# A three-engine score pipeline on one core: one more tile buffer, small steps moved between VectorE, ScalarE and GpSimd, and a new rule for which tiles are summed by DMA

## The chip, the core and the metric

The kernel runs on one core of a Trainium2 chip. The core has TensorE (PE, matrix products into PSUM), VectorE (DVE), ScalarE (ACT), GpSimd (POOL) and SyncE (SP, which here only issues DMAs), each with its own instruction queue, executed in order. They meet through semaphores. The time is device microseconds of one launch; the profile is of one such execution.

## The reference, cut to what matters

`x` is 64 batches of 256 nodes with 128 features, `adj` a 256x256 matrix. Four layers follow each other, each of the form `x = x + layer(relu(layernorm(x)))`. All is float32.

- Layer 0: a gated graph network of five steps. Each step mixes the nodes with `adj`, makes two sigmoid gates and a tanh candidate by 128x128 projections, and updates `h = (1 - z) * h + z * hv`.
- Layer 1: a Chebyshev product of `h`, `h @ adj` and a second hop with `Theta1`, then bias and relu.
- Layer 2: `(adj @ h + h) @ weight + bias`, divided by its norm per node.
- Layer 3: additive attention. For every pair of nodes (i, j) and all 256 channels it needs

```
pre  = s1[i] + s2[j] + b_lin
e    = sum over channels of leaky_relu(pre, 0.2) * a  + adj[i, j]
attn = softmax over j of e
out  = sigmoid(attn @ h)
```

The attention scores are nearly all of the elementwise work: 64 x 256 x 256 pairs with 256 channels each.

## The kernel before, in words

Batches are taken two at a time (32 pairs, `NB` = 2; the two batches of the first pair are started apart, "alone"). Three kinds of work are interleaved.

**Fronts** (`front`, one for each pair) do layers 0 to 2 and the preparation of layer 3. A front is a chain of small steps, each a Python generator's `yield` with the engine that does it. `norm` is the layer normalisation, called four times a front: statistics on VectorE, `1/sqrt(var + eps)` by two instructions on GpSimd (`inverse_root`, L391 and L392), the product -mean * that on VectorE (L469), and the scaled relu on ScalarE (L473). Each of the five recurrent steps has a tanh candidate on ScalarE (L601), `d - hT` on GpSimd (L605) and two updates on VectorE (L608, L612). Near its end a front makes the per-node value `s1o` on VectorE (L741) out of a small tile that VectorE has transposed (L739), and two rows, `lin` and `s2o`, that go to DRAM and come back spread over the partitions.

**Tiles.** The leaky relu is brought to a minimum or a relu of `s1[i] + s2[j]`. A slot is four rows i for both batches of a pair; there are 64 slots a pair, 2048 in all (`NSLOT`). Every slot needs two tiles of 128x2048 float32, one for each half of the 256 channels. The first half (k = 0) is made by VectorE in one instruction (L934) or by GpSimd in eight (L951); the second (k = 1) by ScalarE in eight (L946) or by GpSimd. The tiles live in a ring of 13 buffers, `rl0` to `rl12`. PE scores a tile with eight short matmuls recorded at L1010 (`score`), which add the channels with signs into a PSUM bank, and frees its buffer.

**Joined slots.** In 3 of 10 slots (`SHARE`, list `JOINED`: 614 of 2048, spread evenly to the last) the second half is always made by GpSimd, and a DMA that GpSimd issues (`add_pair`, L971) adds it into the first half's tile. PE then scores the sum once instead of two tiles. The buffer of the second half is free again when the DMA has landed, and the sum can be scored from then on.

**Tails** (`tail`, 64 of them: each half pair of 32 slots that has been scored) do the softmax: VectorE adds `min(s2o, s1o)` to the PSUM scores (L806), GpSimd adds the row `lin` (L818; VectorE in the last tail, L814), VectorE takes the maximum (L822), ScalarE the exponential (L826), PE transposes and multiplies by `h3`, VectorE inverts the sum (L846), ScalarE does the tanh that stands for the sigmoid (L851), and GpSimd the last two steps, `0.5 * o + 0.5` (L856) and `+ x3` (L857; VectorE in the last tail). Then SP sends the tile out.

**The order** of every engine's instructions is fixed when the program is built, by a planner in Python at the end of the function. It keeps a clock for each engine, gives each step an assumed duration (`ran`), and always extends the engine that is furthest behind: a step of a tail first, then one of a front, then, on PE a score and elsewhere a tile (on GpSimd an addition before a tile). So a tile goes to whichever engine has time. A front may not run ahead of a due time tied to the number of scores done:

```
due = STEPS_OF_FRONT * (scored[0] / (2 * SLOTS) - (key - 2)) / SPREAD
if CHAINS[key][2] > due + AHEAD:
```

so front `key` starts when the scores of pair `key - 2` begin and is spread over `SPREAD` = 1.7 pairs of scoring. The planner takes a DMA addition to last 6.6 us from its issue, and at least 5.3 us after the one before. At run time the engines keep the planned order, and wait where the plan was too early.

Of the kernel before, what the change touches and what calls it, by code (L numbers as in the profile page):

```python
# [14 lines left out]
P = 128  # L15
# [6 lines left out]
MOST_POSITIVE = -MOST_NEGATIVE  # L22
PE, DVE, ACT, POOL = ENGINES = (mybir.EngineType.PE, mybir.EngineType.DVE, mybir.EngineType.Activation, mybir.EngineType.Pool)
SLOTS = 64
SHARE = (3, 10)
AHEAD_OF = 2
LOW = 1
ISSUE, ADDED, LANDED, SLACK = 0.65, 5.3, 6.6, 0.3

# [2 lines left out]
def kernel(  # L32
# [122 lines left out]

    ident = const.tile([P, P], F32, name="ident")
    make_identity(nc, ident)
    place = work.tile([P, N], mybir.dt.int32, name="place", bufs=1)
    nc.gpsimd.iota(place, pattern=[[1, N]], base=0, channel_multiplier=0)
    feature = work.tile([P, NE], mybir.dt.int32, name="feature", bufs=1)  # L160
    nc.gpsimd.iota(feature, pattern=[[P, NE]], base=0, channel_multiplier=1)
# [13 lines left out]
    braw = const.tile([P, 5], F32, name="braw")  # L175
    for k, v in enumerate((w3_b, w4_b, w5_b, u3_b, u5_b)):
        nc.scalar.dma_start(braw[:, k:k + 1], v.rearrange("(p o) -> p o", o=1))
    th_raw = const.tile([P, 5, D], F32, name="th_raw")
    nc.sync.dma_start(th_raw, theta.rearrange("(k f) o -> f k o", f=P))
    w2 = const.tile([P, D], F32, name="w2")  # L180
    nc.sync.dma_start(w2, l2_weight)
# [18 lines left out]
    u3t, w4t, w3t, w5t = (wts[:, k] for k in range(4))  # L200
    w34 = const.tile([P, P], F32, name="w34")
    u5t = const.tile([P, P], F32, name="u5t")
    gate_b = const.tile([P, 3], F32, name="gate_b")
    bz, br, bh = gate_b[:, 0:1], gate_b[:, 1:2], gate_b[:, 2:3]
    th = th_raw[:, 0:3, :]
    win = const.tile([P, 63], F32, name="win")
    win_n = const.tile([P, 63], F32, name="win_n")
    w1 = const.tile([P, N], F32, name="w1")
# [6 lines left out]
    def first_constants():  # L215

        for c in range(NC):
            yield PE, 6.0, 1
            b = take()
            for k in range(NC):  # L220
                nc.tensor.transpose(b[0][:, k * P:(k + 1) * P], adj_n[:, k, c * P:(c + 1) * P], ident)
            t = ran(PE, 0.4, 6.0, b[1])
            yield DVE, t
            nc.vector.tensor_copy(adj_t[:, c, :], b[0][:, 0:N])
            t = ran(DVE, 0.35, t)
            spare.append([b[0], t])
# [228 lines left out]
    def norm(src, since, h):  # L455

        nb = src.shape[1]
        stats = work.tile([P, nb * NC, 3], F32, name="stats", bufs=4)
        mv = work.tile([P, nb * NC, 2], F32, name="mv", bufs=4)
        s, h = rows_of(src), rows_of(h)[:, :, 0:D]  # L460
        yield DVE, since
        for k in range(0, nb * NC, 2):
            nc.vector.bn_stats(stats[:, k:k + 2, :].rearrange("p k s -> p (k s)"), s[:, k:k + 2, :].rearrange("p k d -> p d k"))
        t = ran(DVE, STATS[nb], since)
        yield POOL, t
        inverse_root(mv[:, :, 1], stats[:, :, 2], 1.0 / D, OP.mult, LN_EPS, OP.add)
        t = ran(POOL, 1.45, t)
        yield DVE, t
        nc.vector.scalar_tensor_tensor(mv[:, :, 0], stats[:, :, 1], -1.0, mv[:, :, 1], op0=OP.mult, op1=OP.mult)  # L469
        t = ran(DVE, 0.1, t)  # L470
# [9 lines left out]
    def front(p, batches):  # L480
# [55 lines left out]
        for step in range(STEPS):  # L536
# [61 lines left out]
                t = ran(DVE, ELEMENTS[nb], t)  # L598
                spare.append([pv[0], t])
            else:  # L600
                nc.scalar.activation(d, seen(pv), AF.Tanh, bias=bh, scale=1.0)  # L601
                t = ran(ACT, TANH[nb], t)
                spare.append([pv[0], t])
                yield POOL, t
                nc.gpsimd.tensor_sub(d, d, hT)  # L605
                t = ran(POOL, 1.3, t)
            yield DVE, max(t, t_z)
            nc.vector.scalar_tensor_tensor(seen(pr), seen(pr), 1.0, d, op0=OP.add, op1=OP.mult)  # L608
            t = ran(DVE, ELEMENTS[nb], t, t_z)
# [84 lines left out]
        t = ran(POOL, 1.35, t)  # L694

        yield DVE, t, 0, lambda: p < 2 or (p - 2, NC - 1) in TAILED
        x3 = kept("x3", [NC, D])
# [7 lines left out]
        h3 = kept("h3", [NC, D + 1])  # L705
        nc.gpsimd.memset(h3[:, :, :, D:D + 1], 2.0)
        t = yield from norm(x3, t, h3)
        yield PE, t, 1
        b = take()
        to_feature(b[0], h3)  # L710
        t = ran(PE, TURN[nb], t, b[1])
        yield ACT, t
        hT = kept("hT3", [N])
        nc.scalar.copy(hT, seen(b))
        t_hT = ran(ACT, COPY[nb], t)
        spare.append([b[0], t_hT])
# [16 lines left out]
        quarter = work.tile([P, P], F32, name="quarter", bufs=2)  # L733
# [4 lines left out]
        turned = work.tile([P, P], F32, name="turned", bufs=2)  # L738
        nc.vector.transpose(turned[:, 0:cols], quarter[:, 0:cols])  # L739
        s1o = kept("s1o", [NC])  # L740
        nc.vector.tensor_scalar(s1o.rearrange("p b c -> p (b c)"), turned[:, 2:cols:32], b_odd, None, op0=OP.add)  # L741
        ran(DVE, 0.65, t)
# [56 lines left out]
    def tail(u, pe, since):  # L799
# [3 lines left out]
        yield DVE, max(since, ops["t_lin"])  # L803
        sc = feat("sc", **SHORT)
        for k, (b, c) in enumerate(across(u)):
            nc.vector.scalar_tensor_tensor(sc[:, k, :], ops["s2o"][:, b, :], ops["s1o"][:, b, c:c + 1], pe[k], op0=OP.min, op1=OP.add)  # L806
        t = ran(DVE, 0.8, since, ops["t_lin"])
        used = banks_of.pop(u)
        spare.append([used, t])
        end = u == (NPAIR - 1, NC - 1)  # L810
        more = lin.to_broadcast([P, NB, N]) if ops["alone"] else lin
        if end:
            yield DVE, max(t, ops["t_lin"])
            nc.vector.tensor_add(sc, sc, more)  # L814
            t = ran(DVE, ELEMENTS[2], t, ops["t_lin"])
        else:
            yield POOL, max(t, ops["t_lin"])
            nc.gpsimd.tensor_add(sc, sc, more)  # L818
            t = ran(POOL, 1.3, t, ops["t_lin"])
# [26 lines left out]
        nc.vector.reciprocal(rs, po[:, :, D])  # L846
        t = t_s = ran(DVE, 0.15, t)
        yield ACT, t
        o = work.tile([P, NB, D], F32, name="o")
        for k in range(NB):  # L850
            nc.scalar.activation(o[:, k, :], po[:, k, 0:D], AF.Tanh, scale=rs[:, k:k + 1])  # L851
        t = ran(ACT, 0.5, t, t_s)
        spare.append([bank[0], t])
        yield DVE if end else POOL, t
        e = nc.vector if end else nc.gpsimd
        e.tensor_scalar(o, o, 0.5, 0.5, op0=OP.mult, op1=OP.add)  # L856
        e.tensor_add(o, o, x3[:, 0] if ops["alone"] else x3[:, :, u[1], :])  # L857
        ran(DVE, 0.6, t) if end else ran(POOL, 1.2, t)
# [274 lines left out]
```

## Time and profile before

| what | value |
|---|---|
| median of 3 runs | 4924.24 us (4917.30 to 4930.92) |
| the profiled execution | 4930.46 us, its span 4928.2 us |
| busy PE / DVE / ACT / POOL | 97% / 96% / 94% / 95% of the span |
| tiles made by DVE / ACT / POOL | 1817 / 1261 / 1018 |
| joined slots, DMA additions | 614, median 7.8 us from issue to landing |
| granted TensorE clock, mean | 0.993 |

The profiled execution is 6.2 us over the median, and 2.3 us of it lie outside its span. Tiles are counted from instructions: one at L934 is a tile, eight at L946 or at L951 are one. In the groups of instructions a duration is from an instruction's start to its end. ScalarE, GpSimd and PE start the next before the last has ended, so the cost of one in a stream is read from the timeline: the length of an unbroken stretch by the number of instructions in it.

### The profile page before, as it was taken

What the parts mean: (1) busy time and instruction counts of PE and PEld (TensorE: products, weight loads), DVE (VectorE), ACT (ScalarE), POOL (GpSimd) and SP (SyncE); (2) the same over time, 40 slices, a digit from 0 to 9 for tenths busy, and PEclk for the clock granted to TensorE, in tenths of its full rate; (3) what the DMA queues carried; (4) which work ended last, traced back from release to release, by engine and by line L of the source; (5) the groups of instructions that cost most, each with busy time, mean ns of one, the idle gap of its engine ahead of it and who ended that gap; (6) DMA issues with size and microseconds to landing.
All of it is one profiled execution on the core that took longest, in us unless ns stands there. A gap on an engine that the chain in (4) does not pass through costs nothing.

```text
span 4928.2 us, 134012 instructions
## 1 busy us (share of the span) xinstructions
PE 4768.4 (97%) x52471; PEld 1739.2 (35%) x52471; DVE 4713.3 (96%) x3389; ACT 4643.9 (94%) x12142; POOL 4670.5 (95%) x9473
## 2 busy tenths in 40 slices
PE   9999999999999999999999999999999999999987
PEld 4333333333333333333333333333333333333322
DVE  5999999999999999999999999999999999999998
ACT  6999999999999989999999999999999999999998
POOL 3999999999999999999999999999999999999997
PEclk9999999999999999999999999999999999999999
DMA  1666766767767666776776666777767767767677
GB/s 40 137 141 132 151 138 132 148 136 146 144 134 149 138 141 138 143 147 134 145 152 137 142 140 138 148 143 143 144 130 147 148 139 144 144 137 143 143 155 148
DMA packets 133540, 687.45 MB, mean 139 GB/s; under 512 B 15144, under 2 KB 50344, under 8 KB 54312
## 3 DMA queue, kind: packets, MB, share of 16 engines
q0 software_dynamic: 88416, 643.86, 65.3%
q1 hardware_dynamic: 43768, 35.01, 2.3%
q8 instruction: 410, 6.72, 0.5%
q14 instruction: 226, 1.85, 0.1%
q10 hardware_dynamic: 720, 0.00, 0.0%
HBM read 26.48 MB, written 8.52 MB: 7 GB/s over the span
## 4 chain that ended last, share of the span: by engine, by line
PE 31%; POOL 18%; DVE 12%; DMA 7%; ACT 6%; issue 4%; POOLq 0%; ACTq 0%; DVEq 0%
PE bank L1010 19%; POOL rl L951 14%; PE bank L397 11%; DVE rl L934 10%; DMA rl<-rl 7%; ACT rl L946 5%; POOL rl L971 2%; POOL d L605 1%; PE bank L428 1%; POOL mv L392 1%; DVE mv L469 0%; DVE hT L612 0%; PE bank L420 0%; DVE bank L608 0%; POOL sc L818 0%
## 5 line engine op out<-in xcount | busy, mean ns | idle before, releaser
L934 DVE TENSOR_TENSOR rl<-s1a,bank 128x2048 f32<-128x2048 f32 x1817 | 4064.2, 2277 | 100.3 <-DMA rl<-rl 59.2
L946 ACT ACTIVATE rl<-bank,s1b 128x256 f32<-128x256 f32 x10088 | 4047.8, 819 | 113.6 <-DMA rl<-rl 62.8
L951 POOL TENSOR_SCALAR rl<-s2n,s1b 128x256 f32<-128x256 f32 x6296 | 2966.0, 668 | 50.6 <-DMA rl<-rl 19.2
L1010 PE MATMUL bank<-rl,win_n 128*32 128x512 f32 x17768 | 2211.3, 596 | 56.0 <-DVE rl L934 28.0
L1010 PE MATMUL bank<-rl,win 128*32 128x512 f32 x10088 | 1321.9, 597 | 0.0
L1010 PEld LDWEIGHTS bank<-rl,win_n 128*32 128x32 f32 x17768 | 557.2, 110 | 1215.1 <-issue 981.7
L951 POOL TENSOR_SCALAR rl<-s2c,s1a 128x256 f32<-128x256 f32 x1848 | 874.8, 643 | 7.1 <-DMA rl<-rl 2.5
L971 POOL DMA_DIRECT2D rl<-rl x614 | 575.6, 944 | 29.0 <-DVE rl L934 14.8
L1010 PEld LDWEIGHTS bank<-rl,win 128*32 128x32 f32 x10088 | 323.4, 110 | 655.5 <-issue 532.1
L397 PE MATMUL bank<-mT,wts 128*32 128x512 f32 x2480 | 326.2, 594 | 1.6 <-ACT mT L521 1.3
L397 PE MATMUL bank<-adj_t,h 128*32 128x256 f32 x4960 | 300.5, 381 | 7.5 <-ACT h L623 6.4
L605 POOL TENSOR_TENSOR d<-d,hT 128x512 f32<-128x512 f32 x155 | 228.7, 1475 | 37.8 <-ACT d L601 37.8
L397 PEld LDWEIGHTS bank<-adj_t,h 128*32 128x32 f32 x4960 | 159.6, 110 | 178.7 <-issue 46.6
L473 ACT ACTIVATE h<-x,mv 128x128 f32<-128x128 f32 x376 | 176.2, 720 | 13.5 <-DVE mv L469 13.2
L565 ACT ACTIVATE bank<-bank,gate_b 128x512 f32<-128x512 f32 (+1 forms) x165 | 148.5, 900 | 19.4 <-PE bank L397 14.3
L397 PE MATMUL bank<-mT,w 128*32 128x512 f32 x1240 | 163.3, 593 | 3.6 <-ACT bank L565 3.6
L397 PE MATMUL bank<-rh,u5t 128*32 128x512 f32 x1240 | 163.2, 592 | 2.3 <-DVE rh L569 2.3
L588 ACT ACTIVATE bank<-bank,gate_b 128x512 f32<-128x512 f32 (+1 forms) x165 | 154.0, 934 | 9.5 <-PE bank L397 9.4
L397 PE MATMUL bank<-hT,wts 128*32 128x512 f32 x1240 | 162.6, 593 | 0.0
L521 ACT COPY mT<-bank 128x512 f32<-128x512 f32 x155 | 137.1, 885 | 26.8 <-PE bank L397 24.8
L428 PE MATMUL bank<-ident,hT 128*128 128x128 f32 x620 | 101.7, 287 | 57.4 <-DVE hT L612 54.4
L601 ACT ACTIVATE d<-bank,gate_b 128x512 f32<-128x512 f32 x155 | 149.3, 963 | 3.6 <-PE bank L397 3.6
(204 smaller groups left out, 3494.8 us busy)
## 6 DMA issues: line engine op xcount, KB each, us to landing
rl<-rl POOLq DMA_DIRECT2D x614, 1024.0 KB, 7.8
rows<-row SPq DMA_DIRECT2D x31, 512.0 KB
xin<-in_x_dram SPq DMA_DIRECT2D x64, 128.0 KB
out_dram<-o SPq DMA_DIRECT2D x64, 128.0 KB
row<-quarter SPq DMA_DIRECT2D x62, 2.0 KB
rows<-row SPq DMA_DIRECT2D x2, 256.0 KB
w_raw<-in_L_gnn_w_w_dram SPq DMA_DIRECT2D x3, 128.0 KB
th_raw<-in_L_gnn_Theta_dram SPq DMA_DIRECT2D x1, 320.0 KB
```

The costliest lines, as they stand in the source:

```text
L397: nc.tensor.matmul(o[g:g + 32], w[:, g:g + 32], t, start=start, stop=stop, skip_group_check=True)
L428: nc.tensor.transpose(pt[:, b, c, :], ht[:, b, c * P:(c + 1) * P], ident)
L473: nc.scalar.activation(h[:, k, :], s[:, k, :], AF.Relu, bias=mv[:, k, 0:1], scale=mv[:, k, 1:2])
L565: nc.scalar.activation(seen(r), seen(pr), AF.Tanh, bias=br, scale=0.5)
L588: nc.scalar.activation(seen(pr), seen(pr), AF.Tanh, bias=bz, scale=0.5)
L601: nc.scalar.activation(d, seen(pv), AF.Tanh, bias=bh, scale=1.0)
L605: nc.gpsimd.tensor_sub(d, d, hT)
L934: nc.vector.tensor_tensor(t, rows.to_broadcast(whole), ops["s2a"].unsqueeze(1).to_broadcast(whole), op=OP.min)
L946: nc.scalar.activation(t[:, g, b, :], other(ops["s2p"][0], b), AF.Relu, bias=rows[:, g, b], scale=-1.0)
L951: nc.gpsimd.tensor_scalar(t[:, part, b, :], other(ops["s2n" if k else "s2c"], b), rows[:, part, b], MOST_NEGATIVE, op0=OP.min, op1=OP.max)
L971: nc.gpsimd.dma_start(out=t.rearrange("p g b n -> p (g b n)"), in_=z.rearrange("p g b n -> p (g b n)"), accum_op=OP.add)
L1010: nc.tensor.matmul(pe[g * 32:(g + 1) * 32, :], w[:, 31 - r:63 - r], flat(t[:, g]), start=False, stop=(left[u] == 0), skip_group_check=True)
```

## The change

- The ring has 14 tile buffers. Room for it: two set-up tiles (`place`, `th_raw`) lie in the first ring buffer until it is used, `th` becomes a tile of its own, two small tiles (`quarter`, `turned`) have one buffer instead of two, and the attention's turned input uses the `hT` ring of four instead of its own pair.
- Joined slots are 1 of 3 among the first 1952 slots, and none among the last 96: 650 instead of 614.
- `norm`: the sign change of the mean is a reduction over one element on VectorE, right behind the statistics, and the product is on GpSimd behind `inverse_root`. A step to VectorE and back is gone.
- `s1o` is a ScalarE activation (identity with bias) instead of a VectorE one.
- The recurrent candidate is made with its sign turned, so that GpSimd adds instead of subtracts, and the update has -0.5 for 0.5.
- `tail`: L806's result goes back into PSUM, and VectorE adds `lin` out of PSUM, for all tails. The tanh goes into PSUM, and one VectorE instruction does `0.5 * o + x3`. For this, GpSimd adds 0.5 to `x3` once a front, after the last `norm`.
- `SPREAD` is 1.8, and some assumed durations differ.

```diff
-SHARE = (3, 10)
+SHARE = (1, 3)
+ALONE = 96
+    tiles = [[relu_pool.tile([P, 4, NB, N], F32, name=f"rl{k}", bufs=1), 0.0] for k in range(14)]
+    scratch = tiles[0][0].rearrange("p g b n -> p (g b n)")
-    tiles = [[relu_pool.tile([P, 4, NB, N], F32, name=f"rl{k}", bufs=1), 0.0] for k in range(13)]
-    JOINED = [n for n in range(NSLOT) if (n + 1) * SHARE[0] // SHARE[1] > n * SHARE[0] // SHARE[1]]
+    JOINED = [n for n in range(NSLOT - ALONE) if (n + 1) * SHARE[0] // SHARE[1] > n * SHARE[0] // SHARE[1]]
...
+        nc.vector.tensor_reduce(mv[:, :, 0], stats[:, :, 1:2], AX.X, OP.add, negate=True)
         inverse_root(mv[:, :, 1], stats[:, :, 2], 1.0 / D, OP.mult, LN_EPS, OP.add)
-        t = ran(POOL, 1.45, t)
-        yield DVE, t
-        nc.vector.scalar_tensor_tensor(mv[:, :, 0], stats[:, :, 1], -1.0, mv[:, :, 1], op0=OP.mult, op1=OP.mult)
+        nc.gpsimd.tensor_mul(mv[:, :, 0], mv[:, :, 0], mv[:, :, 1])
...
-                nc.scalar.activation(d, seen(pv), AF.Tanh, bias=bh, scale=1.0)
+                nc.scalar.activation(d, seen(pv), AF.Tanh, bias=bh_n, scale=-1.0)
-                nc.gpsimd.tensor_sub(d, d, hT)
+                nc.gpsimd.tensor_add(d, d, hT)
-            nc.vector.scalar_tensor_tensor(hT_new, seen(pr), 0.5, hT, op0=OP.mult, op1=OP.add)
+            nc.vector.scalar_tensor_tensor(hT_new, seen(pr), 0.5 if alone else -0.5, hT, op0=OP.mult, op1=OP.add)
...
         t = yield from norm(x3, t, h3)
+        yield POOL, t
+        nc.gpsimd.tensor_scalar(x3, x3, 0.5, None, op0=OP.add)
-        hT = kept("hT3", [N])
-        nc.scalar.copy(hT, seen(b))
+        hT, t_hT = copied("hT", b, t, bufs=4)
...
-        nc.vector.tensor_scalar(s1o.rearrange("p b c -> p (b c)"), turned[:, 2:cols:32], b_odd, None, op0=OP.add)
+        nc.scalar.activation(s1o.rearrange("p b c -> p (b c)"), turned[:, 2:cols:32], AF.Identity, bias=b_odd, scale=1.0)
...
-            nc.vector.scalar_tensor_tensor(sc[:, k, :], ops["s2o"][:, b, :], ops["s1o"][:, b, c:c + 1], pe[k], op0=OP.min, op1=OP.add)
+            nc.vector.scalar_tensor_tensor(pe[k], ops["s2o"][:, b, :], ops["s1o"][:, b, c:c + 1], pe[k], op0=OP.min, op1=OP.add)
+        nc.vector.tensor_add(sc, by_feature(used), lin.to_broadcast([P, NB, N]) if ops["alone"] else lin)
-            nc.gpsimd.tensor_add(sc, sc, more)
...
-            nc.scalar.activation(o[:, k, :], po[:, k, 0:D], AF.Tanh, scale=rs[:, k:k + 1])
+            nc.scalar.activation(po[:, k, 0:D], po[:, k, 0:D], AF.Tanh, scale=rs[:, k:k + 1])
+        nc.vector.scalar_tensor_tensor(o, po[:, :, 0:D], 0.5, x3[:, 0] if ops["alone"] else x3[:, :, u[1], :], op0=OP.mult, op1=OP.add)
-        e.tensor_scalar(o, o, 0.5, 0.5, op0=OP.mult, op1=OP.add)
-        e.tensor_add(o, o, x3[:, 0] if ops["alone"] else x3[:, :, u[1], :])
...
-    STEPS_OF_FRONT, SPREAD, AHEAD = 109, 1.7, 2
+    STEPS_OF_FRONT, SPREAD, AHEAD = 109, 1.8, 2
```

More of the change, by code (lines that the diff above doesn't have):

```diff
@@ L157 @@
     make_identity(nc, ident)
-    place = work.tile([P, N], mybir.dt.int32, name="place", bufs=1)
+    place = scratch[:, 0:N].bitcast(mybir.dt.int32)
     nc.gpsimd.iota(place, pattern=[[1, N]], base=0, channel_multiplier=0)
@@ L177 @@
         nc.scalar.dma_start(braw[:, k:k + 1], v.rearrange("(p o) -> p o", o=1))
-    th_raw = const.tile([P, 5, D], F32, name="th_raw")
+    th_raw = scratch[:, N:N + 5 * D].rearrange("p (k o) -> p k o", k=5)
     nc.sync.dma_start(th_raw, theta.rearrange("(k f) o -> f k o", f=P))
@@ L202 @@
     u5t = const.tile([P, P], F32, name="u5t")
-    gate_b = const.tile([P, 3], F32, name="gate_b")
-    bz, br, bh = gate_b[:, 0:1], gate_b[:, 1:2], gate_b[:, 2:3]
-    th = th_raw[:, 0:3, :]
+    gate_b = const.tile([P, 4], F32, name="gate_b")
+    bz, br, bh, bh_n = (gate_b[:, k:k + 1] for k in range(4))
+    th = const.tile([P, 3, D], F32, name="th")
     win = const.tile([P, 63], F32, name="win")
@@ L255, in first_constants @@
         nc.vector.tensor_scalar(gate_b[:, 0:2], gate_b[:, 0:2], 0.5, None, op0=OP.mult)
+        nc.vector.tensor_scalar(bh_n, bh, -1.0, None, op0=OP.mult)
         ran(DVE, 0.3)
@@ L463, in norm @@
             nc.vector.bn_stats(stats[:, k:k + 2, :].rearrange("p k s -> p (k s)"), s[:, k:k + 2, :].rearrange("p k d -> p d k"))
-        t = ran(DVE, STATS[nb], since)
+        nc.vector.tensor_reduce(mv[:, :, 0], stats[:, :, 1:2], AX.X, OP.add, negate=True)
+        t = ran(DVE, STATS[nb], since) + 0.1
         yield POOL, t
         inverse_root(mv[:, :, 1], stats[:, :, 2], 1.0 / D, OP.mult, LN_EPS, OP.add)
-        t = ran(POOL, 1.45, t)
-        yield DVE, t
-        nc.vector.scalar_tensor_tensor(mv[:, :, 0], stats[:, :, 1], -1.0, mv[:, :, 1], op0=OP.mult, op1=OP.mult)
-        t = ran(DVE, 0.1, t)
+        nc.gpsimd.tensor_mul(mv[:, :, 0], mv[:, :, 0], mv[:, :, 1])
+        t = ran(POOL, 1.55, t)
         yield ACT, t
@@ L693, in front @@
         inverse_root(rn, rn, MOST_POSITIVE, OP.min, NORM_EPS * NORM_EPS, OP.max)
-        t = ran(POOL, 1.35, t)
+        t = ran(POOL, 1.35, t) + 0.1
         yield DVE, t, 0, lambda: p < 2 or (p - 2, NC - 1) in TAILED
@@ L707, in front @@
         t = yield from norm(x3, t, h3)
+        yield POOL, t
+        nc.gpsimd.tensor_scalar(x3, x3, 0.5, None, op0=OP.add)
+        ran(POOL, 0.45 if alone else 0.7, t)
         yield PE, t, 1
@@ L712, in front @@
         yield ACT, t
-        hT = kept("hT3", [N])
-        nc.scalar.copy(hT, seen(b))
-        t_hT = ran(ACT, COPY[nb], t)
-        spare.append([b[0], t_hT])
+        hT, t_hT = copied("hT", b, t, bufs=4)
         yield PE, t_hT, 1
@@ L732, in front @@
         yield ACT, t
-        quarter = work.tile([P, P], F32, name="quarter", bufs=2)
+        quarter = work.tile([P, P], F32, name="quarter", bufs=1)
         nc.scalar.copy(quarter[:, 0:cols], b[0][:, 0:cols])
@@ L737, in front @@
         yield DVE, t
-        turned = work.tile([P, P], F32, name="turned", bufs=2)
+        turned = work.tile([P, P], F32, name="turned", bufs=1)
         nc.vector.transpose(turned[:, 0:cols], quarter[:, 0:cols])
+        t_s = ran(DVE, 0.2, t)
+        yield ACT, t_s
         s1o = kept("s1o", [NC])
-        nc.vector.tensor_scalar(s1o.rearrange("p b c -> p (b c)"), turned[:, 2:cols:32], b_odd, None, op0=OP.add)
-        ran(DVE, 0.65, t)
+        nc.scalar.activation(s1o.rearrange("p b c -> p (b c)"), turned[:, 2:cols:32], AF.Identity, bias=b_odd, scale=1.0)
+        ran(ACT, 0.2, t_s)
         row = dram.tile([2, NB * N], F32, name="row", bufs=4)
@@ L805, in tail @@
         for k, (b, c) in enumerate(across(u)):
-            nc.vector.scalar_tensor_tensor(sc[:, k, :], ops["s2o"][:, b, :], ops["s1o"][:, b, c:c + 1], pe[k], op0=OP.min, op1=OP.add)
+            nc.vector.scalar_tensor_tensor(pe[k], ops["s2o"][:, b, :], ops["s1o"][:, b, c:c + 1], pe[k], op0=OP.min, op1=OP.add)
         t = ran(DVE, 0.8, since, ops["t_lin"])
+        yield DVE, t
         used = banks_of.pop(u)
+        nc.vector.tensor_add(sc, by_feature(used), lin.to_broadcast([P, NB, N]) if ops["alone"] else lin)
+        t = ran(DVE, ELEMENTS[2], t)
         spare.append([used, t])
[L810 to L817, printed above, removed]
-            nc.gpsimd.tensor_add(sc, sc, more)
-            t = ran(POOL, 1.3, t, ops["t_lin"])
         yield DVE, t
@@ L848, in tail @@
         yield ACT, t
+        for k in range(NB):
+            nc.scalar.activation(po[:, k, 0:D], po[:, k, 0:D], AF.Tanh, scale=rs[:, k:k + 1])
+        t = ran(ACT, 0.5, t, t_s)
+        yield DVE, t
         o = work.tile([P, NB, D], F32, name="o")
-        for k in range(NB):
-            nc.scalar.activation(o[:, k, :], po[:, k, 0:D], AF.Tanh, scale=rs[:, k:k + 1])
-        t = ran(ACT, 0.5, t, t_s)
+        nc.vector.scalar_tensor_tensor(o, po[:, :, 0:D], 0.5, x3[:, 0] if ops["alone"] else x3[:, :, u[1], :], op0=OP.mult, op1=OP.add)
+        t = ran(DVE, 0.36, t)
         spare.append([bank[0], t])
-        yield DVE if end else POOL, t
-        e = nc.vector if end else nc.gpsimd
-        e.tensor_scalar(o, o, 0.5, 0.5, op0=OP.mult, op1=OP.add)
-        e.tensor_add(o, o, x3[:, 0] if ops["alone"] else x3[:, :, u[1], :])
-        ran(DVE, 0.6, t) if end else ran(POOL, 1.2, t)
         p, k = u
```

## The prediction

> **What bounds the kernel now.** I read first the page's busy shares, then windows by stage, then the groups of instructions for what stands before the tiles, and last the timeline for prices and for the end.
>
> ```profile
> PE 4768.4 (97%) x52471; PEld 1739.2 (35%) x52471; DVE 4713.3 (96%) x3389; ACT 4643.9 (94%) x12142; POOL 4670.5 (95%) x9473
> ...
> 2000.00:3000.00 1000.00, 978.78 (x10728) 355.50 (x10720) 969.68 (x688) 956.59 (x2500) 976.01 (x1975) 1.00 0.70 143
> 4700.00:4800.00 100.00, 85.91 (x808) 26.70 (x800) 97.17 (x61) 99.94 (x273) 98.91 (x208) 0.97 0.80 164
> 4850.00:4900.00 50.00, 39.94 (x376) 11.38 (x372) 48.97 (x27) 50.00 (x141) 49.74 (x106) 1.00 0.78 159
> ```
>
> A window row has busy PE, PE's weight loads, DVE, ACT, POOL, then clock, DMA share, GB/s. No engine alone is the bound: in the middle all four are 96 to 98% busy. From 4700 us on (the fronts end at 4747) the three tile makers are full and PE is 80 to 86% busy: there a score saved is worth nothing.
>
> ```profile
> L934 DVE TENSOR_TENSOR rl<-s1a,bank 128x2048 f32<-128x2048 f32 x1817 | 4064.2, 2277 | 100.3 <-DMA rl<-rl 59.2
> L946 ACT ACTIVATE rl<-bank,s1b 128x256 f32<-128x256 f32 x10088 | 4047.8, 819 | 113.6 <-DMA rl<-rl 62.8
> L951 POOL TENSOR_SCALAR rl<-s2n,s1b 128x256 f32<-128x256 f32 x6296 | 2966.0, 668 | 50.6 <-DMA rl<-rl 19.2
> L1010 PE MATMUL bank<-rl,win_n 128*32 128x512 f32 x17768 | 2211.3, 596 | 56.0 <-DVE rl L934 28.0
> ```
>
> The makers' idle time ahead of a tile is mostly for a buffer, held by an addition or by PE; PE's idle time ahead of a score is for a tile. Both sides wait for the other in turn. The chain of waits says the same: PE 31%, the makers 36% together (POOL 18, DVE 12, ACT 6), DMA 7%.
>
> Prices in a stream, from unbroken stretches (start, length, engine, instructions), the first in the chain of waits, the others in the timeline:
>
> ```profile
> 1087.21 10.30 PE bank L1010 x96
> ...
> 2498.27 11.07 DVE L934 TENSOR_TENSOR rl<-s1a,bank 128x2048 f32<-128x2048 f32 x5
> ...
> 2500.70 0.90 POOL L971 DMA_DIRECT2D rl<-rl  x1
> ...
> 2501.33 7.32 POOL L951 TENSOR_SCALAR rl<-s2n,s1b 128x256 f32<-128x256 f32 x16
> ...
> 2506.80 6.00 ACT L946 ACTIVATE rl<-bank,s1b 128x256 f32<-128x256 f32 x16
> ```
>
> A score is eight matmuls, 8 x 10.30/96 = 0.86 us of PE. A tile is 11.07/5 = 2.21 us of DVE, 6.00/2 = 3.00 of ACT, 7.32/2 = 3.66 of POOL; together they make 0.452 + 0.333 + 0.273 = 1.06 tiles a us. An addition keeps POOL 0.63 us (2500.70 to 2501.33).
>
> **Scores.** Joined slots go from 614 to 650. Before, 585 lay in the first 1952 slots, so there it is 65 more: 65 x 0.86 = 56 us off PE. In the last 96 it is 29 fewer: 25 us more for PE, in some 215 us. The three windows from 4700 to 4900 leave PE 14, 7 and 10 us idle, so that is hidden; if that idle time can't be used, it costs at most those 25 us.
>
> **Small steps.** DVE loses L469 (62.7 us in all) and L741 (20.5). Both are mostly waiting: L469's median is 166 ns, its mean 493, its longest 6596, for 4 elements a partition. DVE gains 132 one-element reductions (nearest row L469's median: 22 us), 63 additions of `lin` (L814, the same form on DVE, 0.692: 44) and 63 output steps (128x256 out of PSUM, L569's short form 0.424: 27): 93 for 83. Idle time ahead of L469 (16 us) and of L822 for POOL (8) goes too. DVE is 15 us better off.
>
> POOL loses L818 (87.4), L856 (25.8) and L857 (46.2): 159 us. It gains 132 products of four elements, between L391's 0.195 (26 us in all) and L392's power at 1.03 (136); I take 0.195, since two-input additions grow with size (0.733 for 256 elements, 1.387 for 512) and leave next to nothing for four. It gains 33 additions to `x3`, 128x512: L856 took 0.409 for 256 and L391 0.195 for four, so about 0.62, 20 us (0.41 to 1.39: 14 to 46); and 36 DMA issues, 23 us (at their mean duration 0.944, 34). POOL sheds 159 - 69 = 90 us; at the worst prices it takes on 57. Add for subtract I cost at nothing; if L818's mean against L605's (1.387, 1.475) were the operation's, 155 x 0.088 = 14 us more come off.
>
> ACT gains 33 small activations: 0.2 us, the shortest `quarter` copy, makes 7 us; at that copy's mean of 0.69, 23. The tanh into PSUM costs nothing more: L565 into PSUM has 0.929, L601 into SBUF 0.963.
>
> In tiles: POOL 90/3.66 = 24.6, DVE 15/2.21 = 6.8, ACT -7/3.00 = -2.3: 29 tiles, 27 us. At the worst, -57/3.66 - 10/2.21 - 23/3.00 = -28 tiles, 26 us lost; at the best 31 gained. Some 5 of the 27 lie in the end.
>
> New waits: POOL's addition to `x3` waits for ACT's L473, which still reads it, with tile parts queued behind; ACT's `s1o` waits for DVE's transpose; DVE's output step waits for ACT's tanh, as POOL's L856 did (6.2 us in all), now with 2.2 us tiles behind. Each is planned for when it is due, and I cost them at 0, at most the 20 us that L856 and L469 idled so (6.2 and 13.4). PSUM banks of the tails stay taken about 0.6 us longer, 128 times. PE's waits put down to L851, now the last reader of such a bank, are 5 us in all, so I take 0, at most 5.
>
> **A rule and the rows.** The Trainium skill, SBUF — State Buffer, Who interferes with whom, says that a VectorE instruction with two inputs in SBUF contends with a GpSimd instruction that reads SBUF. L469 has its two inputs there, and its 6.6 us agree; all that VectorE gains has one input in SBUF or none, so by this rule none of it should have a tail of long ones. Against the change stands Perfetto Trace Analysis, Identifying the Most-Contended Engine: judge PE's headroom by its weight loads, not by its matmul busy time. They are 35% busy here, so PE would have room, the saved scores would bring 0, and the sum would lose what the scores bring. I follow the stretch of 96 matmuls without a gap, each holding PE 0.107 us.
>
> **Both together.** In the middle PE is relieved by 56 us and the makers by 22. Where two sides wait in turn the gain lies between; by the chain's shares, 31 to 36, it is 0.46 x 56 + 0.54 x 22 = 38 us.
>
> **The 14th buffer.** Makers idled 100 + 114 + 58 us before tiles, 90 each. One more on 13, less what the additions take: two buffers for 7.8 us every 7.9 us is 2.0 before, 2.2 after. I take a fifth of 90 off: 18. The ends are 0 and 90.
>
> **The end.** Before, DVE's last tile ends at 4908.0 and the last two scores wait for additions:
>
> ```profile
> 4910.76 3.64 PE L1010 MATMUL bank<-rl,win_n 128*32 128x512 f32 x16 [3.65 <-DMA rl<-rl]
> 4915.05 1.85 PE L1010 MATMUL bank<-rl,win_n 128*32 128x512 f32 x8 [0.65 <-DMA rl<-rl]
> ```
>
> Unjoined, scoring is over some 2 us after the last tile, at 4910 instead of 4917: 6 us. With the 5 of the 27 it is 11. In the start only the hop in `norm` goes, about 1 us, under what I can price.
>
> Sum: 38 + 18 + 11 = 67 us off the profiled execution's 4930.5: 4863. That execution is 0.13% over the median, so against the median 4857.
>
> **Rivals.** *PE's relief is worth nothing* (the makers bind): 22 + 5 + 6, with a third of the buffer's share, 39: 4885. For it: DVE at 96 to 97% with no row that lightens it much. Against: 100 us of that engine's idle time is for buffers.
>
> *All comes through*: 56 + 5 + 6 and half of 90, 112: 4812. For it: the makers' idle time is of the kind that a buffer ends. Against: they are 96% busy.
>
> *Late additions, slower.* The middle gets an addition every 150/21.3 = 7 us instead of 7.9, at a faster pace somewhat less. In the end of this trace they come every 6.7 us, and land later than in the middle:
>
> ```profile
> rl<-rl POOLq DMA_DIRECT2D x21, 1024.0 KB, 8.8
> ...
> rl<-rl POOLq DMA_DIRECT2D x128, 1024.0 KB, 7.9
> ```
>
> (window 4750 to 4890, then 2000 to 3000). The planner assumes 6.6. PE's queue is in order, and all scores and front steps behind a late sum wait. PE and its loads waited 27 + 59 us for additions, 0.14 us each. My gain is gone when that grows by 67/650, to 0.24; at 0.31 the 0.17 more are 110 us, and it is 4924 - 67 + 110 = 4967. Against: with 14 buffers a sum need not be scored soon, and at 4750 to 4890 the makers stay 98% full all the same.
>
> *No difference*: the dear prices, 0.46 x 56 - 0.54 x 26 = 12 in the middle and 6 in the end, and additions 0.03 us later each, 20: 4926, with nothing from the buffer.
>
> One thing could also pinch: a front is now spread over 1.8 pairs of 2. By the count of scores done, `s1a` (L785), its last step, ended 1.73 to 1.76 into its pair of pairs; now about 1.81, while 14 buffers let tiles run at most 14/109 = 0.13 ahead, to 1.87. It holds, with some 9 us to spare.
>
> **How the numbers follow.** Forecast 0.5 (4857; its own range 4825 to 4890: the buffer between 0 and 50), makers bind 0.16, all comes through 0.13, late additions 0.13, no difference 0.08. A measurement here tells 0.3%, 15 us, from nothing. Faster: the first three, 0.79 less 0.01; same 0.08; slower 0.14. The range, 4800 to 4930, leaves out the late additions and a little on the other side.
>
> **What would show it.** Right: about 27570 matmuls at L1010 for 27856 (3446 scores); in the middle DVE's and ACT's idle time for buffers down by a fifth or more; L951's count up by some 20 tiles' worth of eight; PE over 90% busy after 4700, and no wait for an addition ahead of the last scores. The product on POOL at 0.2 and the reductions at 0.17 without long ones. Wrong: PE's waits for additions above 150 us, products near 1 us, or tile makers idle at each pair's beginning for `s1a`.

## The result, and the profile after

The changed kernel takes 4888.5 us (median of 4, 4887.5 to 4889.6) against 4923.8 beside it: ratio 0.9928, 95% interval 0.9911 to 0.9945, 35 us less. The forecast was 67 us less, 4857, with a range of 4800 to 4930. The profiled execution took 4887.5 us, its span 4885.3.

First the page of the changed kernel, with the rows that answer to those of before (L930 was L934, L942 L946, L947 L951, L967 L971, L1006 L1010):

```profile
PE 4730.2 (97%) x52183; PEld 1750.7 (36%) x52183; DVE 4677.1 (96%) x3462; ACT 4643.9 (95%) x12151; POOL 4712.9 (96%) x9669
...
L930 DVE TENSOR_TENSOR rl<-s1a,bank 128x2048 f32<-128x2048 f32 x1797 | 4014.4, 2279 | 56.3 <-DMA rl<-rl 41.5
L942 ACT ACTIVATE rl<-bank,s1b 128x256 f32<-128x256 f32 x10064 | 3954.1, 685 | 70.2 <-DMA rl<-rl 32.2
L947 POOL TENSOR_SCALAR rl<-s2n,s1b 128x256 f32<-128x256 f32 x6320 | 3085.7, 841 | 21.0 <-DMA rl<-rl 6.9
L1006 PE MATMUL bank<-rl,win_n 128*32 128x512 f32 x17504 | 2193.0, 594 | 47.3 <-DMA rl<-rl 36.8
...
rl<-rl POOLq DMA_DIRECT2D x650, 1024.0 KB, 8.4
```

GpSimd is busy for longer than before, 4713 us against 4671, but it also made 23 tiles more: 1041 for 1018, close to the 24.6 of the forecast. At 3.66 us each they are 84 us, so its other work fell by some 42 us (an estimate from these numbers), where the forecast had 90. The makers' idle time ahead of tiles has fallen by more than was forecast, from 272 us to 157 (56 + 70 + 21 + 10 at the second L947 row), and yet the time fell by only half of the forecast.

The mean granted TensorE clock rose from 0.993 to 0.998. By these means PE lost some 34 us of full clock before and some 10 after (an estimate: 0.007 of 4928, 0.002 of 4885). The forecast has no term for this, and no run tells what it is worth. The times don't follow it: the kernel of experiment 1 below has 0.999 and is 23 us slower than the changed kernel, that of experiment 7 has 0.996 and is 23 us faster.

The windows of the changed kernel, with columns as before:

```profile
2000.00:3000.00 1000.00, 972.12 (x10684) 355.85 (x10680) 971.12 (x698) 959.86 (x2511) 986.48 (x2017) 1.00 0.78 159
...
4700.00:4800.00 100.00, 99.81 (x944) 35.47 (x937) 98.61 (x56) 99.37 (x273) 99.48 (x221) 1.00 0.03 9
```

In the middle GpSimd is now the fullest engine, 98.6% (97.6 before), and PE has gone from 97.9% to 97.2. After 4700 us, where PE had stood idle for a seventh of the time, all four are full and the DMA engines are nearly idle (a share of 0.03). The last scores of the timeline:

```profile
4867.55 1.06 PE L1006 MATMUL bank<-rl,win_n 128*32 128x512 f32 x8 [0.27 <-DVE rl L930]
4868.43 6.53 PE L1006 MATMUL bank<-rl,win 128*32 128x512 f32 x32
```

VectorE's last tile ends at 4867.5 and ScalarE's at 4873.9. PE scores on without a wait for an addition and is done at 4875.0, 1.1 us after the last tile, where the forecast said some 2.

What the moved steps cost is in the groups of instructions of the changed kernel:

```profile
L713 POOL TENSOR_SCALAR x<-x 128x512 f32<-128x512 f32 x31 | 46.7, 1507 | 2.4
...
L853 DVE SCALAR_TENSOR_TENSOR o<-bank,x 128x256 f32<-128x256 f32 x64 | 26.8, 419 | 1.7 <-ACT bank L849 1.6
...
L473 POOL TENSOR_TENSOR mv<-mv 128x4 f32<-128x4 f32 x124 | 24.6, 199 | 9.7
...
L469 DVE TENSOR_REDUCE mv<-stats 128x4 f32<-128x4 f32 x124 | 19.6, 158 | 4.2
```

The product (0.199), the reduction (0.158) and the output step (0.419) have the forecast's prices, and so has the row's addition on VectorE (L816, 0.683 for 0.692). The addition to `x3` has not: 1.507 us where I took 0.62, over even the upper end of 1.39.

### The profile page after: what moved, and what is told of

It is laid out like the page before. It is cut to its first block, busy times and chain, and to the rows that moved or that the text cites. A ratio compares the mean times of both kernels' runs of the same rounds, so it can differ in the third digit from the quotient of the medians.

```text
span 4885.3 us, 133365 instructions
## 1 busy us (share of the span) xinstructions
PE 4730.2 (97%) x52183; PEld 1750.7 (36%) x52183; DVE 4677.1 (96%) x3462; ACT 4643.9 (95%) x12151; POOL 4712.9 (96%) x9669
## 4 chain that ended last, share of the span: by engine, by line
PE 30%; POOL 26%; DVE 21%; ACT 9%; DMA 9%; issue 6%; POOLq 0%; DVEq 0%; ACTq 0%
POOL rl L947 19%; PE bank L1006 18%; DVE rl L930 17%; PE bank L402 10%; DMA rl<-rl 9%; ACT rl L942 7%; POOL rl L967 3%; POOL d L609 2%; PE bank L433 1%; POOL mv L397 1%; DVE hT L616 1%; DVE bank L612 1%; ACT h L477 1%; POOL x L713 1%; DVE rh L573 0%
## 5 line engine op out<-in xcount | busy, mean ns | idle before, releaser
L930 DVE TENSOR_TENSOR rl<-s1a,bank 128x2048 f32<-128x2048 f32 x1797 | 4014.4, 2279 | 56.3 <-DMA rl<-rl 41.5
L942 ACT ACTIVATE rl<-bank,s1b 128x256 f32<-128x256 f32 x10064 | 3954.1, 685 | 70.2 <-DMA rl<-rl 32.2
L947 POOL TENSOR_SCALAR rl<-s2n,s1b 128x256 f32<-128x256 f32 x6320 | 3085.7, 841 | 21.0 <-DMA rl<-rl 6.9
L1006 PE MATMUL bank<-rl,win_n 128*32 128x512 f32 x17504 | 2193.0, 594 | 47.3 <-DMA rl<-rl 36.8
L1006 PE MATMUL bank<-rl,win 128*32 128x512 f32 x10064 | 1333.5, 594 | 0.0
L947 POOL TENSOR_SCALAR rl<-s2c,s1a 128x256 f32<-128x256 f32 x2008 | 986.1, 765 | 9.6 <-DMA rl<-rl 5.0
L1006 PEld LDWEIGHTS bank<-rl,win_n 128*32 128x32 f32 x17504 | 566.0, 110 | 1188.8 <-issue 918.8
L967 POOL DMA_DIRECT2D rl<-rl x650 | 717.9, 1127 | 9.4 <-DVE rl L930 2.9
L1006 PEld LDWEIGHTS bank<-rl,win 128*32 128x32 f32 x10064 | 330.3, 110 | 637.9 <-issue 512.4
L609 POOL TENSOR_TENSOR d<-d,hT 128x512 f32<-128x512 f32 x155 | 233.5, 1510 | 23.8 <-ACT d L605 23.7
L477 ACT ACTIVATE h<-x,mv 128x128 f32<-128x128 f32 x376 | 163.1, 574 | 52.4 <-POOL mv L473 52.1
L612 DVE SCALAR_TENSOR_TENSOR bank<-bank,d 128x512 f32<-128x512 f32 x155 | 107.8, 695 | 64.5 <-POOL d L609 63.8
L569 ACT ACTIVATE bank<-bank,gate_b 128x512 f32<-128x512 f32 (+1 forms) x165 | 134.5, 815 | 23.0 <-PE bank L402 15.0
L402 PEld LDWEIGHTS bank<-mT,wts 128*32 128x32 f32 x2480 | 82.3, 110 | 184.3 <-issue 149.7
L397 POOL TENSOR_TENSOR mv<-mv,minus_half 128x4 f32<-128x4 f32 (+1 forms) x132 | 133.9, 1015 | 11.0
```

The costliest lines, as they stand in the source:

```text
L397: nc.gpsimd.tensor_tensor(t, t, minus_half[:, 0:t.shape[1]], op=OP.pow)
L402: nc.tensor.matmul(o[g:g + 32], w[:, g:g + 32], t, start=start, stop=stop, skip_group_check=True)
L569: nc.scalar.activation(seen(r), seen(pr), AF.Tanh, bias=br, scale=0.5)
L609: nc.gpsimd.tensor_add(d, d, hT)
L930: nc.vector.tensor_tensor(t, rows.to_broadcast(whole), ops["s2a"].unsqueeze(1).to_broadcast(whole), op=OP.min)
L942: nc.scalar.activation(t[:, g, b, :], other(ops["s2p"][0], b), AF.Relu, bias=rows[:, g, b], scale=-1.0)
```

## The experiments

Each is timed beside the kernel before, and its ratio to that is what counts: differences in microseconds are differences of ratios on 4924. A time that stands alone is the run's own median; the kernel before took 4925 to 4939 us beside them. Two orders of the same instructions can differ in time by themselves, by some 12 us as the third and the fifth suggest; pairs that share one order are the clean ones: the changed kernel and the third, the third and the sixth, the fifth and the twelfth, and the changed kernel and the fourth up to 4674 us. All other pairs differ in their order too.

**1. The old share of joined slots, in the changed kernel.**

```diff
-SHARE = (1, 3)
+SHARE = (3, 10)
```

> The changed kernel (4888.5 us) with 3 of 10 slots joined instead of 1 of 3, still none in the last 96: 585 additions instead of 650, so PE gets 65 x 0.86 = 56 us of scores back in the middle and GpSimd loses 65 x 0.63 = 41 us of issues, 11 tiles, 10 us of the makers' time. Theory 'the makers bind': the 56 us were worth nothing, so this is the same or a little faster, 4876 to 4890. Theory 'PE counted, and the gain was eaten by dearer steps': 0.46 x 56 - 0.54 x 10 = 20 us slower, about 4909.

0.9974 (0.9963 to 0.9984): 4911.3 us, 23 us slower than the changed kernel, about twice what an order may do by itself. PE hardly waits for tiles any more, 7 us ahead of these scores where it was 47, and the makers wait 260 us, where it was 157:

```profile
L1006 PE MATMUL bank<-rl,win_n 128*32 128x512 f32 x18256 | 2250.3, 594 | 7.3 <-DVE rl L930 3.9
```

So "the makers bind", whose forecast of 4885 happened to be near the result, falls: PE's 56 us in the middle are worth 23 us even against 41 us of GpSimd's time given back. By the rule of the Trainium skill (Perfetto Trace Analysis, Identifying the Most-Contended Engine), with weight loads 36% busy PE would have had room for them; here the measurement decides.

**2. Thirteen buffers in the changed kernel.**

```diff
-... for k in range(14)]
+... for k in range(13)]
```

> The changed kernel with 13 tile buffers instead of 14. The forecast's term says 18 us slower, 4906. Theory 'the makers bind': the makers' idle time ahead of tiles (56 + 70 + 31 us now, 100 + 114 + 58 before) is what ends in a shorter time, so the buffer is worth up to (272 - 157)/3 = 38 us, 4926. Theory 'the additions eat the buffer': no more than 5 us, 4893.

0.9934 (0.9922 to 0.9947): 3 us slower, within the error. The makers wait for tiles again, in the groups of this kernel 92 + 79 + 36 + 8 = 215 us, 58 more than with 14:

```profile
L942 ACT ACTIVATE rl<-bank,s1b 128x256 f32<-128x256 f32 x10160 | 4015.2, 705 | 78.7 <-DMA rl<-rl 55.9
L930 DVE TENSOR_TENSOR rl<-s1a,bank 128x2048 f32<-128x2048 f32 x1790 | 4000.2, 2277 | 91.6 <-DMA rl<-rl 50.6
L947 POOL TENSOR_SCALAR rl<-s2n,s1b 128x256 f32<-128x256 f32 x6224 | 2996.5, 772 | 36.3 <-PE bank L1006 13.4
L947 POOL TENSOR_SCALAR rl<-s2c,s1a 128x256 f32<-128x256 f32 x2064 | 1001.0, 721 | 8.1 <-DMA rl<-rl 4.2
```

But the waits behind GpSimd are shorter by about as much, 56 us. In the changed kernel ScalarE's L477 waited 65.6 us for the product and VectorE's L612 63.8 us for `d + hT` (both rows stand at experiment 12); here it is

```profile
ACT h L477 <- POOL mv L473: 25.0, 31, 2.9
DVE bank L612 <- POOL d L609: 48.3, 52, 2.5
```

So it fits that the time which the buffer saves ahead of tiles comes back as waits for GpSimd. It is not shown alone, since the order changed too.

**3. The addition to `x3` with two operations in the instruction.** Nothing else differs, and the order of all engines is the same.

```diff
-nc.gpsimd.tensor_scalar(x3, x3, 0.5, None, op0=OP.add)
+nc.gpsimd.tensor_scalar(x3, x3, 1.0, 0.5, op0=OP.mult, op1=OP.add)
```

> The changed kernel with GpSimd's addition to x3 written as times 1.0, plus 0.5, two operations in the instruction as L856 of the kernel before had, instead of one. If the single-operation form is what makes 128x512 take 1.507 us where 0.62 was forecast, it falls to about 0.62 here: 33 x 0.89 = 29 us off GpSimd. Theory 'the makers bind': 29/3.66 = 8 tiles, 7 us, 4881; if GpSimd's lateness itself is on the path, up to 29, 4860. If the form is not the cause the duration stays at 1.5 and the time at 4888.

0.9878 (0.9864 to 0.9891): 4863.6 us, 25 us faster. The groups of instructions of this kernel have

```profile
L713 POOL TENSOR_SCALAR x<-x 128x512 f32<-128x512 f32 x31 | 19.3, 624 | 2.5 <-ACT h L477 0.2
```

so 31 x 0.883 + 2 x 0.46 = 28 us less on GpSimd, of which 25 arrive. They aren't shared out over three makers, as the forecast did with all such time (7 us): each engine makes the same tiles in both kernels. The order was fixed with 0.7 us assumed for this step; what exceeds the plan nobody can take over, and the engines that wait for GpSimd wait longer: `d + hT` held up L612 on VectorE for 63.8 us in the changed kernel, for 47.5 in this one.

**4. Slots joined to the very end.**

```diff
-ALONE = 96
+ALONE = 0
```

> The changed kernel with 1 of 3 slots joined to the end (682 additions, 32 more, all in the last 96). The forecast's term for the end says 11 us slower, 4899; the pace of the last two pairs in the two profiles (242 us after, 259 before) says up to 17, 4905. The last scores wait for additions again, by some 4 us. Theory 'PE is short in the end too': it gets 32 x 0.86 = 28 us of scores less, and the time is the same or less.

0.9951 (0.9939 to 0.9964): 4900.0 us, 11 us slower than the changed kernel. The forecast had 11 us for the end too, but only 6 of them for the joins, the other 5 for the small steps; so what this run measures had a price of 6, and that it comes to 11 does not confirm the sum's term; nor are 6 ruled out, since the two intervals overlap. The last score waits for an addition again, by 2.04 us in its timeline:

```profile
4884.77 1.07 PE L1006 MATMUL bank<-rl,win_n 128*32 128x512 f32 x8 [2.04 <-DMA rl<-rl]
```

**5. The planner told of the slow addition**, which stays slow.

```diff
-ran(POOL, 0.45 if alone else 0.7, t)
+ran(POOL, 0.9 if alone else 1.55, t)
```

> The changed kernel with the slow one-operation addition to x3 kept (1.507 us), but with the planner told so: 1.55 us assumed instead of 0.7. With the two-operation form, whose order of instructions is the same as the changed kernel's, 28 us less on GpSimd had brought 25. Theory 'time that the plan does not know of is paid in full, time that it knows is spread over the three makers': the 28 us cost 8 tiles, 7 us, over 4863.6, so about 4871. Theory 'GpSimd's time is what counts, planned or not': it stays at 4888.

0.9853 (0.9839 to 0.9866): 4856.5 us, faster than expected, and ahead of the two-operation kernel by 0.25%, though it does 28 us more on GpSimd. Against the changed kernel it is 37 us for the same work in an order planned with the true duration. That the plan's knowing is what helps fits, but it isn't shown alone: 37 us are more than the 28 that the plan did not know of, so a part is probably the order's doing, and this is one order. By 0.25% two orders can differ by some 12 us for reasons that I don't follow up. Smaller differences between orders aren't read below.

**6. The tanh into SBUF**, on experiment 3's kernel, in its order.

```diff
-nc.scalar.activation(po[:, k, 0:D], po[:, k, 0:D], AF.Tanh, scale=rs[:, k:k + 1])
+nc.scalar.activation(o[:, k, :], po[:, k, 0:D], AF.Tanh, scale=rs[:, k:k + 1])
...
-nc.vector.scalar_tensor_tensor(o, po[:, :, 0:D], 0.5, x3..., op0=OP.mult, op1=OP.add)
+nc.vector.scalar_tensor_tensor(o, o, 0.5, x3..., op0=OP.mult, op1=OP.add)
```

> The two-operation kernel (4863.6 us) with the output's tanh written to SBUF as in the kernel before, and the last step of VectorE reading it there. In the changed kernel the second of the two tanh instructions waits until the first has ended, since both write one PSUM bank: from the first's start to the next instruction's the pair takes 0.99 us, before 0.51; 64 x 0.48 = 31 us of ScalarE that the plan does not know of. The order of instructions is the same. Theory 'unplanned time on any full engine is paid nearly in full': up to 25 us faster, 4839. Theory 'only GpSimd's counts, ScalarE has 5% idle': 0 to 7 faster, 4857 to 4864. VectorE's last step then has two inputs in SBUF, as L469 had, whose excess of 0.33 us each would make 21 us: by this the gain is eaten, 4864 or more.

0.9947 (0.9933 to 0.9961): 4903.8 us, 0.69% or 34 us slower than experiment 3. VectorE's output step, now with both inputs in SBUF, went from 26.8 us in all to 99.7:

```profile
L854 DVE SCALAR_TENSOR_TENSOR o<-o,x 128x256 f32<-128x256 f32 x64 | 99.7, 1558 | 1.3 <-ACT o L850 1.3
```

73 us that no plan knew of on VectorE, less what ScalarE's pair no longer waits (by the expectation's estimate 31), cost 34. Here is the longest of them, with GpSimd beside it (timeline of this kernel, VectorE, then GpSimd):

```profile
4659.23 7.12 DVE L854 SCALAR_TENSOR_TENSOR o<-o,x 128x256 f32<-128x256 f32 x1
...
4659.34 4.00 POOL L947 TENSOR_SCALAR rl<-s2c,s1a 128x256 f32<-128x256 f32 x8
4662.92 4.18 POOL L947 TENSOR_SCALAR rl<-s2n,s1b 128x256 f32<-128x256 f32 x8
4666.64 1.30 POOL L967 DMA_DIRECT2D rl<-rl  x1
```

VectorE stood in an instruction of 0.42 us while GpSimd started sixteen of its own, 0.45 us apart. It was done at 4666.35, behind the start of the last of them and 0.3 us before GpSimd's next instruction, the DMA issue.

**7. The ring and the joins alone**, in the kernel before: 14 buffers with the room made for them, `SHARE` and `ALONE` as in the change, no moved step.

```diff
-SHARE = (3, 10)
+SHARE = (1, 3)
+ALONE = 96
...
-... for k in range(13)]
+... for k in range(14)]
```

> The kernel before with the 14th buffer and the new rule of joined slots, and none of the moved steps. By what undoing has shown (23 us for the joins in the middle, 11.5 for the end, 2.4 for the buffer): 37 us faster than before, 4888, as fast as the whole change, so the moved steps with the slow x3 addition are worth nothing in sum. By the forecast's terms (26 + 18 + 6): 50 us faster, 4875. Theory 'the joins pay only with GpSimd relieved of the tails': GpSimd has 23 us more to do, so 6 us less gain at least, 4895 to 4910.

0.9882 (0.9869 to 0.9896): 4871.1 us, 58 us faster than before and more than the whole change. The forecast's terms for these parts made 50. So the moved steps, in the form that they have here and with the wider spread, take back 23 us.

**8. The 14th buffer alone**, in the kernel before, with the room made for it.

```diff
-... for k in range(13)]
+... for k in range(14)]
```

> The kernel before with the 14th buffer alone. The forecast took 18 us for it: 4907. Taking it from the changed kernel cost 2.4: 4922. If buffers were what the makers lack, up to 90 us: 4840.

0.9939 (0.9927 to 0.9952): 30 us faster. The same buffer is worth 30 us here and 3 in experiment 2, each time with an order of its own.

**9. The tails as before**, in the changed kernel: GpSimd adds the row and does the last two steps, the tanh goes to SBUF, and there is no addition to `x3`.

```diff
-nc.gpsimd.tensor_scalar(x3, x3, 0.5, None, op0=OP.add)
...
-nc.vector.tensor_add(sc, by_feature(used), ... lin)
+nc.gpsimd.tensor_add(sc, sc, more)
...
-nc.vector.scalar_tensor_tensor(o, po[:, :, 0:D], 0.5, x3..., op0=OP.mult, op1=OP.add)
+e.tensor_scalar(o, o, 0.5, 0.5, op0=OP.mult, op1=OP.add)
+e.tensor_add(o, o, x3...)
```

> The changed kernel with the tails as before (GpSimd adds the row, ScalarE's tanh goes to SBUF, GpSimd does the last two steps) and so without the addition to x3. What stays of the moved steps is norm's product, s1o and the sign. GpSimd has 159 - 33 x 1.5 = 109 us more to do than in the changed kernel, 30 tiles, VectorE 71 us less, 32 tiles, and both know it from the plan: as good as nothing. Unplanned time goes: 28 us of x3 on GpSimd and 31 us of the tanh pair on ScalarE. Theory 'unplanned time is paid': 25 us faster than 4888 from x3 alone, 4863, and up to 25 more, 4840. Theory of the forecast (GpSimd relieved is time gained): 4888 - 25 + (159/3.66 - 71/2.21)/1.06 = 4874.

0.9906 (0.9889 to 0.9922): 46 us faster than before, 11 faster than the changed kernel, where 25 and more were expected by the one theory and 14 by the forecast's way. Against experiment 3 the moved tails are worth 14 us (0.9878 to 0.9906, intervals that overlap).

**10. Only the output steps back on GpSimd**, and no addition to `x3`.

```diff
-nc.gpsimd.tensor_scalar(x3, x3, 0.5, None, op0=OP.add)
...
-nc.scalar.activation(po[:, k, 0:D], po[:, k, 0:D], AF.Tanh, scale=rs[:, k:k + 1])
-nc.vector.scalar_tensor_tensor(o, po[:, :, 0:D], 0.5, x3..., op0=OP.mult, op1=OP.add)
+nc.scalar.activation(o[:, k, :], po[:, k, 0:D], AF.Tanh, scale=rs[:, k:k + 1])
+e.tensor_scalar(o, o, 0.5, 0.5, op0=OP.mult, op1=OP.add)
+e.tensor_add(o, o, x3...)
```

> The changed kernel with only the output steps as before (tanh to SBUF, two steps on GpSimd, no addition to x3); VectorE still adds the row out of PSUM. Against the changed kernel GpSimd has 72 - 50 = 22 us more, VectorE 27 less. Theory 'unplanned time is paid': 4863 from x3, and up to 25 us less for the tanh pair that no longer waits, 4838; if ScalarE's 5% of idle time hides the pair's wait, 4863. Theory 'taking the row's addition off GpSimd is what helped': faster than the kernel with the tails wholly as before by 87/3.66/1.06 - 44/2.21/1.06 = 4 us.

0.9903 (0.9889 to 0.9918). Without the slow addition and without the pair's wait it is no faster than experiment 9 and slower than experiment 3, which has that wait. So the pair's 31 us on ScalarE aren't paid in anything like full: my theory that unplanned time counts on any full engine falls for ScalarE, or is hidden under the order's error.

**11. The tanh pair planned at its length**, on experiment 3's kernel.

```diff
-t = ran(ACT, 0.5, t, t_s)
+t = ran(ACT, 0.95, t, t_s)
```

> The two-operation kernel (4863.6 us) with the tanh pair, 0.99 us measured, assumed to take 0.95 in the plan instead of 0.5. The work is the same. Theory 'unplanned time is paid, planned is spread': of the 31 us a third and less remains (31/3.00/1.06 = 10), so up to 15 us faster, 4849. Theory 'ScalarE has room': no change, 4860 to 4867. Another order by itself can shift the time by some us either way.

0.9889 (0.9874 to 0.9904) against experiment 3's 0.9878: no change that can be told. With the tenth it fits that ScalarE has room for these waits; apart from the order it isn't shown.

**12. Experiment 5's order with the short addition.**

```diff
-nc.gpsimd.tensor_scalar(x3, x3, 0.5, None, op0=OP.add)
+nc.gpsimd.tensor_scalar(x3, x3, 1.0, 0.5, op0=OP.mult, op1=OP.add)
...
-ran(POOL, 0.45 if alone else 0.7, t)
+ran(POOL, 0.9 if alone else 1.55, t)
```

> The kernel in which the planner was told 1.55 us for the addition to x3 (ratio 0.9853 to before), now with the addition in its two-operation form, which takes 0.62: the order of instructions is that kernel's, and GpSimd has 28 us less to do, so that much slack. In the changed kernel's own order the same exchange brought 25 us. Theory 'GpSimd lags its plan in other steps too (norm's product takes 0.30 with its gap where the plan adds 0.10, 26 us in all), and slack on it is taken up': 10 to 25 us faster, a ratio of 0.980 to 0.983. Theory 'once planned, the addition was no longer late and nothing waits for it': the same, 0.985.

0.9823 (0.9809 to 0.9836): 4847.3 us, the fastest here, 87 us less than before and 0.3% or 15 us ahead of experiment 5, whose order it has. Its plan reserves 0.9 us too much on GpSimd once a front, and that is taken up. GpSimd was late elsewhere too: the timeline of the changed kernel has, once for each of 132 norms,

```profile
2514.80 0.20 POOL L396 TENSOR_SCALAR mv<-stats 128x4 f32<-128x4 f32 x1
2515.07 1.04 POOL L397 TENSOR_TENSOR mv<-mv,minus_half 128x4 f32<-128x4 f32 x1
2516.19 0.20 POOL L473 TENSOR_TENSOR mv<-mv 128x4 f32<-128x4 f32 x1
2516.49 0.94 POOL L947 TENSOR_SCALAR rl<-s2c,s1a 128x256 f32<-128x256 f32 x2
```

The three hold GpSimd from 2514.80 to 2516.49, 1.69 us where the plan has 1.55: 132 x 0.14 = 18 us. Whether the slack pays for this is not shown. What waits for GpSimd has shrunk; here are the waits of the changed kernel, of experiment 5 and of this one:

```profile
ACT h L477 <- POOL mv L473: 65.6, 51, 3.6
DVE bank L612 <- POOL d L609: 63.8, 66, 2.5
```

```profile
ACT h L477 <- POOL mv L473: 43.0, 32, 3.2
DVE bank L612 <- POOL d L609: 40.3, 53, 1.9
```

```profile
ACT h L477 <- POOL mv L473: 44.9, 32, 3.3
...
DVE bank L612 <- POOL d L609: 33.6, 50, 2.2
```

But the wait for the product fell with the order, from the first to the second, and not with the slack, from the second to the third. The wait for `d + hT` fell with both, by 7 us with the slack. Where the rest of the 15 us comes from stays open.

## Why the prediction was right, and where it was not

The direction, the range and the likeliest case's own range (4825 to 4890) held, the last by 1.5 us, which is luck. The size was off by half: 35 us where 67 were said. By experiment 7 the joins and the ring brought more than the forecast gave them, 58 us for 50; the small steps, which were to help, took 23 of it back.

- **Joined slots and both together.** The sum gave the 56 us of PE a weight of 0.46; less 10 us for the makers, the old share should have cost 20. It cost 23. The mixing by shares of the chain came out, within what an order may do by itself, and the rival "PE's relief is worth nothing", whose number lay nearest to the result, was wrong in its mechanism.
- **The end.** The wait for the last additions went as said. Leaving the last slots apart had a price of 6 us, and 11 were measured, with intervals that overlap. The sum's 11 for the end had 5 from the small steps besides, so that the two elevens agree by chance.
- **The 14th buffer.** 18 us forecast; 30 alone in the kernel before, 3 in the changed kernel. Both lie in my bounds of 0 to 90. A single price was the mistake: it depends on what the makers do with the time, and in the changed kernel, with GpSimd behind its plan, it fits that the waits for GpSimd took it up (experiment 2). Ring and joins together came out at 58 us against 50.
- **Small steps.** This is the step that failed. They were to bring some 17 us (0.54 x 22 in the middle, 5 in the end) and took 23 with the wider spread, by the difference between experiment 7 and the changed kernel. One price failed, "33 additions to `x3`, 128x512: L856 took 0.409 for 256 and L391 0.195 for four, so about 0.62": it took 1.507. The row was of two operations and the new instruction has one; in the two-operation form it takes 0.624, as I had extrapolated. Worse was the spreading of it: I turned GpSimd's microseconds into tiles for three makers, and time that the planner doesn't know of is not shared out so. 28 us of the addition cost 25, not 7. With the short form the moved steps are worth 2 us over ring and joins (0.9878 to 0.9882), nothing that can be told; with slack on GpSimd besides, and in another order, 29 (0.9823).
- **New waits at 0.** Wrong in a place that I had not named: ScalarE's L477 waited 65.6 us for the product on GpSimd; before, it waited 28 us for VectorE's. The step and the hop that are gone come back as a wait behind GpSimd's queue, of a length that goes with the order (25.0 us in experiment 2, 43.0 in experiment 5). The tanh pair's wait was missed too, and costs little.
- **Late additions.** Additions landed in 8.4 us (7.8 before), and PE and its loads waited 36.8 + 76.5 us for 650 of them, 0.17 each. The price from which this rival decides was 0.24; it was not reached. The price itself was no good measure: in experiment 2 these waits were 50.8 + 134.0 us, 0.28 each, and the gain was still there but for 3 us.
- **The rule on two SBUF inputs.** It held in both directions: none of the instructions that VectorE gained has a long tail (their longest are 0.163, 0.691 and 0.425 us), and giving one of them its second input in SBUF cost 73 us of VectorE's time.

What stays open: why experiments 9 and 10, without the slow addition, are not as fast as experiment 7; the moved product, `s1o`, the sign and the wider spread are what they share and it lacks. It was not taken apart, and the difference, 0.24%, is near the error between orders.

## What to carry to other kernels

Where the order of every engine is written out ahead, price a change by the plan first: time that the plan doesn't know of can be paid nearly in full by the engine that lags, here 25 us of 28 on GpSimd in one order. On VectorE it was 34 of 73 us, with up to 31 given back on ScalarE (experiment 6). How far time that the plan knows is spread over the engines was not measured by itself; in experiment 12's order, which had the time in its plan, dropping the same 28 us still brought 15. Take a price from a row of the same form, not only of the same operation and size, and put the measured duration back into the plan. And an engine's idle time is worth its ending only where the next thing that it waits for is not late as well: one buffer was worth 30 us in one kernel and 3 in the other.

## What the runs showed of the hardware

- On GpSimd a tensor-scalar instruction of one operation (add a constant, 128x512 float32) took 1.507 us, and with two (times 1.0, plus 0.5) 0.624; for 128x256 it is 0.868 and 0.406. Whether the missing second operation makes the difference, or the addition as the first one, was not told apart.
- An instruction of VectorE with two inputs in SBUF can be passed over by a whole stream of GpSimd's: 7.12 us for 0.42 us of work, through sixteen instructions. The Trainium skill, SBUF — State Buffer, SBUF: two separate sides, says that of the two whichever starts first has the shared ports for its whole instruction and the other is blocked. In the trace of experiment 6 VectorE was held for far longer than one GpSimd instruction, until the stream of sixteen came to its end.
- Two ScalarE instructions that write different parts of one PSUM bank come with a wait of the second for the first. The pair took from 2382.50 to 2383.45 us, 0.95, in the changed kernel and 0.50 (1194.48 to 1194.98) into SBUF before.
- A subtraction and an addition on GpSimd cost the same: L605 and L609 have a shortest duration of 1.27 and 1.26 us.
